# Four blocks of convolution and attention on one core: the order of the first transfers, |pos| and sign for the first pair on VectorE, the fourth block's norm and transpose ahead of the loop, the dense pair's late sums, and P7 before P3 in the projection

## The chip, the core and the metric

One core of a Trainium2 chip runs the whole program in one launch. The engines are TensorE (PE; its weight loads are listed as PEld), VectorE (DVE), ScalarE (ACT), GpSimd (POOL) and the queue engine SyncE (SP). The metric is the device time of one execution in microseconds; less is better. All arithmetic is in float32.

## What is computed

The input x is 2 x 512 x 32 x 32. Four layers follow one another, each adding to x.

Layer 0 is deformable attention with 8 heads and a dense pair. Per pair of heads (eight pairs: two images, four channel blocks of 128), cut to what matters here:

```python
q = gconv1x1(bn1(x))                              # per head 64 channels
off = tanh(gelu(depthwise_6x6_stride4(q)) @ pw) * 4
kv = grid_sample(bn1(x), key_grid + off)          # 64 keys; k, v = gconv1x1(kv)
pos = grid_q - grid_kv                            # 1024 queries x 64 keys x 2
bias = sign(pos) * log1p(abs(pos))
bias = relu(relu(bias @ w1 + b1) @ w2 + b2) @ w3 + b3
out = softmax(q @ k.T / 8 + bias) @ v
x = x + out_w @ out + out_b
x = x + mlp_w2 @ gelu(mlp_w1 @ bn2(x) + mlp_b1) + mlp_b2
```

Layer 1 is a linear attention. Layers 2 and 3 are group norm, attention with 8 heads over 1024 positions, and a projection that is added to x; layer 3's result is the output.

## The kernel before

x stays in on-chip memory as eight tiles of 128 x 1024 (`xs[b][t]`, image b, channel block t; called x00 to x13 below).

**Start (lines 72 to 177).** `prologue` issues the eight loads of x on SP's queue. `layer0` issues on ACT's queue, in this order: the first block of the q weights (`l0qkv`, L105), `cols` (all per-channel columns: norms, biases, the taps of the depthwise convolution, L106), `grid` (L107), `w2` (L109), the row of w3 (L254), the other k and v weights (L115), the other q weights (L116) and the output weights (L118). The program lets some of these issues wait for the landing of an earlier transfer (SP's third load of x waited 3.4 us for the first q weights), and what is queued behind such an issue on its engine waits as well.

The rest of the start is the first pair's chain (`offsets`, L317): its norm on VectorE (L450, wants x00 and `cols`), its q product (L469), copies of q into a padded tile (L478), the convolution by three engines at once (`first_conv`, L402: GpSimd makes 16 diagonal matrices, PE multiplies by them, ACT and VectorE take the other taps), gelu, tanh, and then `pos` (L367), ACT's Abs, Ln and Sign (L378 to L380) and the product `log` (L382). Into VectorE's queue between `pos` and `log` are placed the folding of |w3| into w2 (L276, L277) and the third part of the generator `last_weights`: `ends`, a matrix with the signs of w3 in four columns (L267, L270; the last product of the bias uses it), and the copy of the row numbers `ys` (L271; the first sampling uses it). Between the steps PE runs dummy products (`warm`, L147).

From `log` the first table is made (`table`, L553: two masked copies on VectorE, L579, spread over all partitions by PE, L586, then x by ACT, L595, and y by VectorE, L596), and from it the first hidden layer h (L618, VectorE). Before the loop, the transposes of the blocks 1 and 2 (normed ahead by GpSimd, L160) and the q of pair 1 are placed. ACT copies each transpose into an `att` tile; `sampled` (L483) takes it from there. For the other pairs `sampled` makes norm, transpose and copy itself, inside the loop (L493).

**Loop (L179 to L208).** 256 quads (16 heads x 8 groups of keys x 2). Each quad: PE multiplies h by w2 (L649, 64 passes), ACT applies Relu (L654), ACT, GpSimd and accumulating DMAs add signed parts, and the result goes into the last product (L681) two quads later. The next pair's steps and the softmax of finished heads are spread over the quads. PE, ACT, VectorE and GpSimd follow the order in which this code is written (`manual_schedule`).

**End of layer 0 and the dense pair.** The last head's softmax (`attend`, L689) alternates on PE with shares of the output projection (`share`, L227). `mlp0` (L824) begins with the norm of image 0 into seven blocks: `norm` makes four and `right_sums` (L803) forms four sums from them, two of which (L807, L808) feed only the products P7 and P4. This part stands outside a written-out order: a planner places its VectorE instructions into the queue by its own estimate of time. Then eight slabs follow in a written order, each with seven block products ("P1 P6 P2 P7 P5 P4 P3", then "P1 P3 P2 P6 P7 P5 P4") whose results VectorE adds up.

**Projection of layers 2 and 3 (`project`, L1572).** Seven products per image in the order P1 P2 P6 P5 P3 P7 P4, each in a place of two PSUM banks. After P6 GpSimd adds u to three blocks of x; P5 adds to two blocks, P3 to one, P7 to two, P4 to one, all on VectorE. In layer 3 each block is stored as soon as it is complete; for image 1, P4 is split into three pieces (L1596 to L1608).

Of the kernel before, what the change touches and what calls it, by code (L numbers as in the profile page):

```python
# [11 lines left out]
F32 = mybir.dt.float32  # L12
AF = mybir.ActivationFunctionType
# [5 lines left out]
P = 128  # L19
B, C, H, W = 2, 512, 32, 32  # L20
N = H * W
CT = C // P
# [32 lines left out]
class Net:  # L55
# [16 lines left out]
    def prologue(self, ctx: ExitStack):  # L72
        nc, io = self.nc, self.io
        const = self.const = self.pool(ctx, "const")
        xpool = self.pool(ctx, "x")
        self.cols = const.tile([P, NCOL], F32, tag="cols", name="cols")
        self.grid = const.tile([P, NGRID], F32, tag="grid", name="grid")
        x_in = io["x"].rearrange("b (t p) h w -> b t p (h w)", p=P)
        self.xs = []
        for b in range(B):  # L80
            self.xs.append([])
            for t in range(CT):
                xt = xpool.tile([P, N], F32, tag=f"x{b}{t}", name=f"x{b}{t}")
                nc.sync.dma_start(xt, x_in[b, t])
                self.xs[b].append(xt)
        self.ident = const.tile([P, P], F32, tag="ident", name="ident")
        make_identity(nc, self.ident)
# [10 lines left out]
    def layer0(self):  # L98
# [3 lines left out]
        with ExitStack() as ctx:  # L102
            keep = self.pool(ctx, "l0")
            self.l0qkv = keep.tile([P, 3, CT, P], F32, tag="qkv", name="qkv")
            nc.scalar.dma_start(self.l0qkv[:, 0, 0], io["l0_qkv"][:, 0, 0])  # L105
            nc.scalar.dma_start(self.cols, io["cols"])  # L106
            nc.scalar.dma_start(self.grid, io["grid"])  # L107
            self.l0w2 = keep.tile([P, P], F32, tag="w2", name="w2")
            nc.scalar.dma_start(self.l0w2, io["cpb_w2"])  # L109
# [31 lines left out]
            with self.tc.manual_schedule(engines=engines):  # L141
# [5 lines left out]
                def warm(n):  # L147
                    for _ in range(n):
                        nc.tensor.matmul(ones_ps[:, 0:P], lhsT=self.all, rhs=self.all, start=True, stop=True)

                warm(13)
                for n, _ in enumerate(self.offsets(pairs[0], 0, ps)):
                    if n == 1:
                        warm(5)
                    elif n == 2:
                        first_tr = self.turn(pairs[0], 0, ps)
                    elif n == 4:
                        warm(11)
                for t in (1, 2):
                    self.normed(pairs[t], t, True)  # L160
                pairs[0]["xT"] = self.fone.tile([P, NB, P], F32, tag="xnT", name="xnT00")
                nc.scalar.copy(pairs[0]["xT"], first_tr)
                front = [self.sampled(pairs[0], 0, ps)]
# [4 lines left out]


                att = [apool.tile([P, N], F32, tag=f"att{t}", name=f"att0_{t}") for t in range(CT)]  # L170
                for t in (1, 2):
                    tr = self.turn(pairs[t], t, ps)
                    pairs[t]["xT"] = att[t].rearrange("p (n c) -> p n c", c=P)
                    nc.scalar.copy(pairs[t]["xT"], tr)
                    if t == 1:
                        self.queries(pairs[1], 1, ps)
                del pairs[2]["xn"]
                held, self.join = [], None
                for i, (u, o, jj) in enumerate(quads):  # L179
                    self.jj = jj  # L180
# [66 lines left out]
    def last_weights(self, keep):  # L247

        nc = self.nc
        self.w3row = keep.tile([P, P], F32, tag="row", name="w3row")
        nc.scalar.dma_start(self.w3row, self.io["cpb_w3"].partition_broadcast(P))  # L254
        yield
        w3 = self.colr("w3r", 4)
        self.magb = keep.tile([P, 4], F32, tag="magb", name="magb")
        nc.vector.scalar_tensor_tensor(self.magb, w3, -1.0, w3, ALU.mult, ALU.max)
        nc.vector.tensor_tensor(self.magb, self.magb, self.colr("b2r", 4), ALU.mult)
        sign = keep.tile([P, 4], F32, tag="sign", name="sign")  # L260
        nc.vector.tensor_scalar(sign, w3, 0.0, 2.0, ALU.is_ge, ALU.mult)
        nc.vector.tensor_scalar(sign, sign, -1.0, None, ALU.add)
        self.flip = keep.tile([P, 3], F32, tag="flip", name="flip")
        nc.vector.tensor_tensor(self.flip, sign[:, 0:3], sign[:, 3:4].to_broadcast([P, 3]), ALU.mult)
        yield
        self.ends = keep.tile([P, 60], F32, tag="ends", name="ends")
        nc.vector.memset(self.ends, 0.0)  # L267
        for k in range(4):
            rows = slice(32 * k, 32 * k + 32)
            nc.vector.tensor_copy(self.ends[rows, 28 + k : 29 + k], sign[rows, 3:4])  # L270
        nc.vector.tensor_copy(self.ys, self.grid[:, G_Y : G_Y + NB])  # L271
        yield

# [43 lines left out]
    def offsets(self, m, bt, ps):  # L317
# [53 lines left out]
            ALU.subtract,  # L371
        )
        yield
        if bt == 0:
            self.fold_weights()
            next(self.weights)
        log = self.fpool.tile([P, 2, W], F32, tag="log", name=f"log{b}{t}")
        nc.scalar.activation(log, pos, AF.Abs)  # L378
        nc.scalar.activation(log, log, AF.Ln, bias=1.0)
        nc.scalar.activation(pos, pos, AF.Sign)  # L380
        yield
        nc.vector.tensor_tensor(log, log, pos, ALU.mult)  # L382
        logs = self.dram.tile([P, 2 * W], F32, tag="logs", name=f"logs{b}{t}")
        nc.sync.dma_start(logs, log.rearrange("p d x -> p (d x)"))
        spots = self.dram.tile([P, 2], F32, tag="spots", name=f"spots{b}{t}")
# [53 lines left out]
        nc.vector.tensor_tensor(conv, conv, acc, ALU.add)  # L439
        yield  # L440

    def normed(self, m, bt, ahead=False):
        nc = self.nc
        b, t = divmod(bt, CT)
        if ahead:
            xn = self.hid2.tile([P, N], F32, tag="h23", bufs=5, name=f"xn{b}{t}")
        else:
            xn = self.fone.tile([P, N], F32, tag="xn", name=f"xn{b}{t}")
        m["xn"] = xn
        (nc.gpsimd if ahead else nc.vector).tensor_scalar(  # L450
            xn, self.xs[b][t], self.s1[:, t : t + 1], self.col("bn1_b", t), ALU.mult, ALU.add
        )

# [99 lines left out]
    def table(self, u, o, pairs, tables):  # L553
# [14 lines left out]
        if u == 0 and o < 2:  # L568
# [8 lines left out]
            for d in range(2):  # L577
# [13 lines left out]
                    stop=True,  # L591
                )
                parts.append(got)
            x = tables["x"][:, :, i : i + 4, :]
            nc.scalar.activation(x, parts[0], AF.Identity, scale=self.col("cpb_w1", 0), bias=self.col("cpb_b1"))  # L595
            nc.vector.tensor_scalar(y, parts[1], self.col("cpb_w1", 1), None, ALU.mult)  # L596
# [205 lines left out]

    def right_sums(self, eng, r):  # L803

        eng.tensor_tensor(r[4], r[1], r[0], ALU.subtract)
        eng.tensor_tensor(r[5], r[3], r[4], ALU.subtract)
        eng.tensor_tensor(r[1], r[3], r[1], ALU.subtract)  # L807
        eng.tensor_tensor(r[6], r[2], r[5], ALU.subtract)  # L808

# [14 lines left out]
    def mlp0(self):  # L824
# [5 lines left out]
        with ExitStack() as ctx:  # L830
# [16 lines left out]
            def norm(b):  # L847

                r = [xpool.tile([P, 2, HF], F32, tag=f"r{i}", name=f"mx{b}{i}") for i in range(7)]
                for i in (0, 3, 2, 1):  # L850
                    for k in range(2):
# [7 lines left out]
                            ALU.add,  # L859
                        )  # L860
                        yield r
                self.right_sums(vec, r)
                yield r

            for xn in norm(0):
# [2 lines left out]
            with self.tc.manual_schedule(engines={getattr(mybir.EngineType, e) for e in ("PE", "Activation", "DVE")}):  # L868
                for n in range(B * CT):
# [11 lines left out]
                    for i, acc in self.seven("P1 P6 P2 P7 P5 P4 P3", ps, w1, lambda r, k: xn[r][:, k, :], f"m1_{n}"):  # L881
# [20 lines left out]
                                gelu(p, 1)  # L902
                        if i == "P5":
                            held = acc
                    for p in range(2):
                        self.right_sums(vec, h[p])
                    following = norm(1) if n == CT - 1 else iter(())
# [540 lines left out]
    def heads_bounded(self, k, ones, data, proj, out):  # L1448
# [7 lines left out]
        with ExitStack() as ctx:  # L1456
# [115 lines left out]
            def project(b):  # L1572
# [15 lines left out]

                us = ap2.tile([P, 2, HF], F32, tag="sum", name=f"pu{k}{b}")
                at = ("a", "b", "even", "a", "b", "even", "a") if b == 0 else ("odd", "even", "b", "odd", "even", "a", "b")  # L1590
                for which, spot in zip(("P1", "P2", "P6", "P5", "P3", "P7", "P4"), at):
                    a, ri = SEVEN[which]
                    acc = place(spot, f"pb{k}{b}{which}")
                    if out is not None and b == 1 and which == "P4":
# [307 lines left out]
```

## Time and profile before

| | us |
|---|---|
| three timed runs | 3351.06, 3352.95, 3353.19 |
| median | 3352.95 |
| the profiled execution's own time | 3351.15 |
| its span, first to last instruction | 3349.3 |
| PE busy | 3336.1 (100%) |
| VectorE busy | 2310.4 (69%) |
| GpSimd busy | 2176.0 (65%) |
| ACT busy | 2056.0 (61%) |
| granted TensorE clock, mean | 1.000 |

The span and all times in the profile come from one profiled execution; what lies outside the span makes 1.85 us of that execution. Times of instructions are counted from the start of the span. Lines of a timeline have start, duration, engine and line of code, operation, output <- input, shape and count, and in brackets how long the engine was idle before and what ended that. A list of waits has total, number and longest wait. An engine named with a q (ACTq, SPq) is its queue of issues. The PE's busy time includes overlapping of successive matmuls. The idle time of PE in the span is 3349.3 - 3336.1 = 13.2 us.

By stage: the start with the first pair's chain takes the first 23 us; the loop runs to about 2005; layer 0's last softmax and projection end at 2033; the dense pair ends at 2417; layer 1 at 2481; layer 2 at 2914; layer 3 takes the rest.

### The profile page before, as it was taken

What the parts mean: (1) busy time and instruction counts of PE and PEld (TensorE: products, weight loads), DVE (VectorE), ACT (ScalarE), POOL (GpSimd) and SP (SyncE); (2) the same over time, 40 slices, a digit from 0 to 9 for tenths busy, and PEclk for the clock granted to TensorE, in tenths of its full rate; (3) what the DMA queues carried; (4) which work ended last, traced back from release to release, by engine and by line L of the source; (5) the groups of instructions that cost most, each with busy time, mean ns of one, the idle gap of its engine ahead of it and who ended that gap; (6) DMA issues with size and microseconds to landing.
All of it is one profiled execution on the core that took longest, in us unless ns stands there. A gap on an engine that the chain in (4) does not pass through costs nothing.

```text
span 3349.3 us, 60380 instructions
## 1 busy us (share of the span) xinstructions
PE 3336.1 (100%) x25318; PEld 1242.6 (37%) x25318; DVE 2310.4 (69%) x2521; ACT 2056.0 (61%) x2173; POOL 2176.0 (65%) x1665
## 2 busy tenths in 40 slices
PE   9999999999999999999999999999999999999999
PEld 4333333333333333333333334444565533455333
DVE  6777777767766677777766665564565578755787
ACT  7887887887886688887888771111121466213662
POOL 6887878877877677878878874333323447634475
PEclk9999999999999999999999999999999999999999
DMA  7777877877777577777888762111000100000001
GB/s 178 158 160 152 160 158 154 160 156 158 160 154 143 119 157 150 161 157 152 160 172 162 159 136 104 38 51 38 1 1 0 38 2 1 14 0 14 1 1 52
DMA packets 102674, 342.67 MB, mean 102 GB/s; under 512 B 12657, under 2 KB 14833, under 8 KB 99313
## 3 DMA queue, kind: packets, MB, share of 16 engines
q0 software_dynamic: 73296, 266.90, 40.8%
q1 hardware_dynamic: 27936, 69.68, 7.2%
q8 instruction: 203, 3.33, 0.4%
q10 hardware_dynamic: 1152, 2.06, 0.2%
q14 instruction: 87, 0.70, 0.1%
HBM read 67.27 MB, written 4.46 MB: 21 GB/s over the span
## 4 chain that ended last, share of the span: by engine, by line
PE 96%; DVE 1%; POOL 1%; issue 1%; DMA 0%; ACT 0%; ACTq 0%; POOLq 0%; DVEq 0%
PE hp L649 51%; PE s L1482 7%; PE o L1511 7%; PE sim L681 3%; PE qk30P L1260 1%; PE qk20P L1260 1%; PE qk31P L1260 1%; PE m_6P L819 1%; PE m_5P L819 1%; PE m_3P L819 1%; PE m_1P L819 1%; PE m_0P L819 1%; PE qk21P L1260 1%; PE m_7P L819 1%; PE m_4P L819 1%; PE m_2P L819 1%
## 5 line engine op out<-in xcount | busy, mean ns | idle before, releaser
L649 PE MATMUL hp<-h,w 128*32 128x512 f32 x16384 | 1794.9, 593 | 0.3 <-ACT h L654 0.3
L618 DVE CUSTOM_DVE_ANT_1 h<-tx,bank 128x1024 f32<-128x1024 f32 (+1 forms) x1028 | 1181.0, 1212 | 310.2 <-PE hp L649 239.1
L654 ACT ACTIVATE h<-hp,magb 128x1024 f32<-128x1024 f32 x1024 | 1120.9, 1111 | 371.3 <-PE hp L649 365.1
L649 PEld LDWEIGHTS hp<-h,w 128*32 128x32 f32 x16384 | 526.9, 110 | 1199.0 <-issue 1148.0
L641 POOL DMA_DIRECT2D h<-h x509 | 451.4, 1024 | 365.6 <-ACT h L660 308.8
L667 POOL TENSOR_TENSOR h<-h,h 128x1024 f32<-128x1024 f32 x255 | 610.3, 2393 | 21.3
L665 POOL TENSOR_SCALAR h<-h,flip 128x1024 f32<-128x1024 f32 x256 | 448.4, 1751 | 0.9 <-ACT h L654 0.9
L1486 ACT ACTIVATE e<-s 128x1024 f32<-128x1024 f32 x256 | 261.8, 1024 | 155.5 <-PE s L1482 151.7
L656 ACT ACTIVATE h<-h,flip 128x1024 f32<-128x1024 f32 x256 | 291.4, 1138 | 0.0
L1482 PE MATMUL s<-q,k 64*64 64x512 f32 x2048 | 265.2, 589 | 0.0
L1511 PE MATMUL o<-e,v 64*64 64x512 f32 x2048 | 265.1, 589 | 0.0
L1493 POOL TENSOR_TENSOR some<-some,e 128x1024 f32<-128x1024 f32 x64 | 160.8, 2513 | 42.5 <-ACT e L1486 38.7
L1491 POOL TENSOR_TENSOR some<-e,e 128x1024 f32<-128x1024 f32 x32 | 75.8, 2367 | 157.8 <-DVE sum L1500 125.6
L658 POOL TENSOR_SCALAR h<-h,flip 128x1024 f32<-128x1024 f32 x128 | 142.9, 1116 | 45.4 <-ACT h L654 44.7
L660 ACT ACTIVATE h<-h,flip 128x1024 f32<-128x1024 f32 x128 | 145.7, 1138 | 0.0
L681 PE MATMUL sim<-h,ends 128*32 128x512 f32 x1024 | 133.3, 592 | 0.0
L1511 PEld LDWEIGHTS o<-e,v 64*64 64x64 f32 x2048 | 78.3, 133 | 141.4 <-issue 135.1
L1482 PEld LDWEIGHTS s<-q,k 64*64 64x64 f32 x2048 | 78.1, 133 | 141.0 <-issue 115.5
L797 POOL TENSOR_TENSOR mlp_w<-mlp_w 128x512 f32<-128x512 f32 x16 | 22.3, 1393 | 161.6 <-DMA mlp_w<-in_mlp_w 161.5
L1496 DVE TENSOR_TENSOR sum<-e,e 128x1024 f32<-128x1024 f32 x32 | 57.4, 1792 | 99.8 <-ACT e L1486 99.8
L878 ACT ACTIVATE mh<-mh,cols 128x512 f32<-128x512 f32 x64 | 46.2, 722 | 124.2 <-DVE mh L896 65.5
L1534 DVE RECIPROCAL r<-r 128x512 f32<-128x512 f32 x32 | 107.3, 3353 | 1.1
(545 smaller groups left out, 3313.6 us busy)
## 6 DMA issues: line engine op xcount, KB each, us to landing
h<-h POOLq DMA_DIRECT2D x509, 512.0 KB, 6.4
lb<-logs SPq DMA_DIRECT2D x63, 512.0 KB, 5.2
mlp_w<-in_mlp_w SPq DMA_DIRECT2D x16, 1024.0 KB, 4.9
x<-in_x SPq DMA_DIRECT2D x8, 512.0 KB, 9.8
qkw<-in_l_qk SPq DMA_DIRECT2D x2, 2048.0 KB, 8.3
out<-x SPq DMA_DIRECT2D x15, 256.0 KB, 2.1
vw<-in_l_v SPq DMA_DIRECT2D x2, 1024.0 KB, 8.0
projw<-in_l_proj SPq DMA_DIRECT2D x2, 1024.0 KB, 4.6
```

Source lines behind the costliest of these rows:

```text
L618: self.nc.vector._custom_dve(TENSOR_ADD_SAT, out=h1[r][:, k, cut, :], in0=x[:, jj, 2 * r + k, :].unsqueeze(1).to_broadcast([P, H // parts, ...
L641: nc.gpsimd.dma_start(to, what, accum_op=ALU.add)
L649: nc.tensor.matmul(hp[rows, cut], lhsT=self.l0w2[:, 32 * q : 32 * q + 32], rhs=h1[k][:, cut], start=True, stop=True)
L654: nc.scalar.activation(y, hp, AF.Relu, bias=self.magb[:, q : q + 1])
L656: nc.scalar.activation(ys[0], ys[0], AF.Copy, scale=self.flip[:, 0:1])
L665: nc.gpsimd.tensor_scalar(y, y, self.flip[:, 2:3], 1.0, ALU.mult, ALU.mult)
L667: (nc.vector if final else nc.gpsimd).tensor_tensor(y, y, ys[2], ALU.add)
L681: nc.tensor.matmul(sims[u][at : at + 32, :], lhsT=self.ends[:, 28 - 4 * o : 60 - 4 * o], rhs=z[jj][:, h * HF : (h + 1) * HF], start=(o == ...
L819: self.nc.tensor.matmul(acc[p], lhsT=w[:, a, k, p * P : (p + 1) * P], rhs=right(r, k), start=k == 0, stop=k == 1)
L1482: nc.tensor.matmul(s[halves[c], par, :], lhsT=ks[p][rows, at : at + DH], rhs=qs[p][rows, cut], start=True, stop=True)
L1486: nc.scalar.activation(e, s, AF.Exp, scale=DH**-0.5)
L1511: nc.tensor.matmul(o[halves[par], r, :], lhsT=v[n // 2][rows, n % 2, at : at + DH], rhs=e[rows, par, :], start=(n == 0), stop=(n == NB - 1),)
```

## The change

- `cols` becomes the first transfer on ACT's queue. The loads of x move from `prologue` into `layer0`, still on SP's queue, and the first block of the q weights goes to SP, between the loads of x00 and x01.
- For the first pair, |pos| is max(-pos, pos) on VectorE, and the sign is made there as 2 (pos >= 0), used as (that - 1) times the logarithm; ACT keeps Ln alone. `ends` (a memset and four copies) goes to GpSimd, and the `ys` copy becomes a step of its own, taken when the second table is made.
- The first run of dummy products has 11 instead of 13. The norms of the blocks 1 and 2 stand earlier in the program on GpSimd.
- Block 3 is normed ahead as well, on VectorE, inside the first table; its transpose and copy go before the loop with those of 1 and 2, and pair 1's q products come after the three transposes.
- The last two sums of the dense pair's first image move from the norm to behind P6 of the first slab.
- In `project`, P7 comes before P3; the places keep their order.

```diff
--- before.py
+++ after.py
@@ -75,13 +75,11 @@
         xpool = self.pool(ctx, "x")
         self.cols = const.tile([P, NCOL], F32, tag="cols", name="cols")
         self.grid = const.tile([P, NGRID], F32, tag="grid", name="grid")
-        x_in = io["x"].rearrange("b (t p) h w -> b t p (h w)", p=P)
         self.xs = []
         for b in range(B):
             self.xs.append([])
             for t in range(CT):
                 xt = xpool.tile([P, N], F32, tag=f"x{b}{t}", name=f"x{b}{t}")
-                nc.sync.dma_start(xt, x_in[b, t])
                 self.xs[b].append(xt)
         self.ident = const.tile([P, P], F32, tag="ident", name="ident")
         make_identity(nc, self.ident)
@@ -102,8 +100,13 @@
         with ExitStack() as ctx:
             keep = self.pool(ctx, "l0")
             self.l0qkv = keep.tile([P, 3, CT, P], F32, tag="qkv", name="qkv")
-            nc.scalar.dma_start(self.l0qkv[:, 0, 0], io["l0_qkv"][:, 0, 0])
+            x_in = io["x"].rearrange("b (t p) h w -> b t p (h w)", p=P)
             nc.scalar.dma_start(self.cols, io["cols"])
+            for bt in range(BP):
+                b, t = divmod(bt, CT)
+                nc.sync.dma_start(self.xs[b][t], x_in[b, t])
+                if bt == 0:
+                    nc.sync.dma_start(self.l0qkv[:, 0, 0], io["l0_qkv"][:, 0, 0])
             nc.scalar.dma_start(self.grid, io["grid"])
             self.l0w2 = keep.tile([P, P], F32, tag="w2", name="w2")
             nc.scalar.dma_start(self.l0w2, io["cpb_w2"])
@@ -148,16 +151,16 @@
                     for _ in range(n):
                         nc.tensor.matmul(ones_ps[:, 0:P], lhsT=self.all, rhs=self.all, start=True, stop=True)
 
-                warm(13)
+                warm(11)
                 for n, _ in enumerate(self.offsets(pairs[0], 0, ps)):
                     if n == 1:
                         warm(5)
                     elif n == 2:
                         first_tr = self.turn(pairs[0], 0, ps)
+                        for t in (1, 2):
+                            self.normed(pairs[t], t, nc.gpsimd)
                     elif n == 4:
                         warm(11)
-                for t in (1, 2):
-                    self.normed(pairs[t], t, True)
                 pairs[0]["xT"] = self.fone.tile([P, NB, P], F32, tag="xnT", name="xnT00")
                 nc.scalar.copy(pairs[0]["xT"], first_tr)
                 front = [self.sampled(pairs[0], 0, ps)]
@@ -168,13 +171,12 @@
 
 
                 att = [apool.tile([P, N], F32, tag=f"att{t}", name=f"att0_{t}") for t in range(CT)]
-                for t in (1, 2):
+                for t in range(1, CT):
                     tr = self.turn(pairs[t], t, ps)
                     pairs[t]["xT"] = att[t].rearrange("p (n c) -> p n c", c=P)
                     nc.scalar.copy(pairs[t]["xT"], tr)
-                    if t == 1:
-                        self.queries(pairs[1], 1, ps)
-                del pairs[2]["xn"]
+                self.queries(pairs[1], 1, ps)
+                del pairs[2]["xn"], pairs[3]["xn"]
                 held, self.join = [], None
                 for i, (u, o, jj) in enumerate(quads):
                     self.jj = jj
@@ -264,10 +266,11 @@
         nc.vector.tensor_tensor(self.flip, sign[:, 0:3], sign[:, 3:4].to_broadcast([P, 3]), ALU.mult)
         yield
         self.ends = keep.tile([P, 60], F32, tag="ends", name="ends")
-        nc.vector.memset(self.ends, 0.0)
+        nc.gpsimd.memset(self.ends, 0.0)
         for k in range(4):
             rows = slice(32 * k, 32 * k + 32)
-            nc.vector.tensor_copy(self.ends[rows, 28 + k : 29 + k], sign[rows, 3:4])
+            nc.gpsimd.tensor_copy(self.ends[rows, 28 + k : 29 + k], sign[rows, 3:4])
+        yield
         nc.vector.tensor_copy(self.ys, self.grid[:, G_Y : G_Y + NB])
         yield
 
@@ -371,15 +374,23 @@
             ALU.subtract,
         )
         yield
+        log = self.fpool.tile([P, 2, W], F32, tag="log", name=f"log{b}{t}")
         if bt == 0:
+
+            nc.vector.scalar_tensor_tensor(log, pos, -1.0, pos, ALU.mult, ALU.max)
+            nc.vector.tensor_scalar(pos, pos, 0.0, 2.0, ALU.is_ge, ALU.mult)
             self.fold_weights()
             next(self.weights)
-        log = self.fpool.tile([P, 2, W], F32, tag="log", name=f"log{b}{t}")
-        nc.scalar.activation(log, pos, AF.Abs)
-        nc.scalar.activation(log, log, AF.Ln, bias=1.0)
-        nc.scalar.activation(pos, pos, AF.Sign)
-        yield
-        nc.vector.tensor_tensor(log, log, pos, ALU.mult)
+            nc.scalar.activation(log, log, AF.Ln, bias=1.0)
+        else:
+            nc.scalar.activation(log, pos, AF.Abs)
+            nc.scalar.activation(log, log, AF.Ln, bias=1.0)
+            nc.scalar.activation(pos, pos, AF.Sign)
+        yield
+        if bt == 0:
+            nc.vector.scalar_tensor_tensor(log, pos, -1.0, log, ALU.add, ALU.mult)
+        else:
+            nc.vector.tensor_tensor(log, log, pos, ALU.mult)
         logs = self.dram.tile([P, 2 * W], F32, tag="logs", name=f"logs{b}{t}")
         nc.sync.dma_start(logs, log.rearrange("p d x -> p (d x)"))
         spots = self.dram.tile([P, 2], F32, tag="spots", name=f"spots{b}{t}")
@@ -439,7 +450,7 @@
         nc.vector.tensor_tensor(conv, conv, acc, ALU.add)
         yield
 
-    def normed(self, m, bt, ahead=False):
+    def normed(self, m, bt, ahead=None):
         nc = self.nc
         b, t = divmod(bt, CT)
         if ahead:
@@ -447,7 +458,7 @@
         else:
             xn = self.fone.tile([P, N], F32, tag="xn", name=f"xn{b}{t}")
         m["xn"] = xn
-        (nc.gpsimd if ahead else nc.vector).tensor_scalar(
+        (ahead or nc.vector).tensor_scalar(
             xn, self.xs[b][t], self.s1[:, t : t + 1], self.col("bn1_b", t), ALU.mult, ALU.add
         )
 
@@ -591,6 +602,10 @@
                     stop=True,
                 )
                 parts.append(got)
+            if o == 0:
+                self.normed(pairs[3], 3, nc.vector)
+            else:
+                next(self.weights)
             x = tables["x"][:, :, i : i + 4, :]
             nc.scalar.activation(x, parts[0], AF.Identity, scale=self.col("cpb_w1", 0), bias=self.col("cpb_b1"))
             nc.vector.tensor_scalar(y, parts[1], self.col("cpb_w1", 1), None, ALU.mult)
@@ -802,8 +817,16 @@
 
     def right_sums(self, eng, r):
 
+        self.first_sums(eng, r)
+        self.second_sums(eng, r)
+
+    @staticmethod
+    def first_sums(eng, r):
         eng.tensor_tensor(r[4], r[1], r[0], ALU.subtract)
         eng.tensor_tensor(r[5], r[3], r[4], ALU.subtract)
+
+    @staticmethod
+    def second_sums(eng, r):
         eng.tensor_tensor(r[1], r[3], r[1], ALU.subtract)
         eng.tensor_tensor(r[6], r[2], r[5], ALU.subtract)
 
@@ -859,7 +882,9 @@
                             ALU.add,
                         )
                         yield r
-                self.right_sums(vec, r)
+                self.first_sums(vec, r)
+                if b > 0:
+                    self.second_sums(vec, r)
                 yield r
 
             for xn in norm(0):
@@ -902,6 +927,8 @@
                                 gelu(p, 1)
                         if i == "P5":
                             held = acc
+                        if i == "P6" and n == 0:
+                            self.second_sums(vec, xn)
                     for p in range(2):
                         self.right_sums(vec, h[p])
                     following = norm(1) if n == CT - 1 else iter(())
@@ -1588,7 +1615,7 @@
 
                 us = ap2.tile([P, 2, HF], F32, tag="sum", name=f"pu{k}{b}")
                 at = ("a", "b", "even", "a", "b", "even", "a") if b == 0 else ("odd", "even", "b", "odd", "even", "a", "b")
-                for which, spot in zip(("P1", "P2", "P6", "P5", "P3", "P7", "P4"), at):
+                for which, spot in zip(("P1", "P2", "P6", "P5", "P7", "P3", "P4"), at):
                     a, ri = SEVEN[which]
                     acc = place(spot, f"pb{k}{b}{which}")
                     if out is not None and b == 1 and which == "P4":
```

## The prediction

> **What bounds the kernel now.** I read the page's busy times and chain first, then the list of waits of the matmul engine, then timelines of the places which those waits name: the first 35 us, a stretch inside the long loop, the end of layer 0, and the last 10 us.
>
> ```profile
> PE 3336.1 (100%) x25318; PEld 1242.6 (37%) x25318; DVE 2310.4 (69%) x2521; ACT 2056.0 (61%) x2173; POOL 2176.0 (65%) x1665
> ...
> PE 96%; DVE 1%; POOL 1%; issue 1%; DMA 0%; ACT 0%; ACTq 0%; POOLq 0%; DVEq 0%
> ```
> PE is without matmuls for only 3349.3 - 3336.1 = 13.2 us. A change gains only where it shortens those 13 us, moves PE work into a stretch where PE waits anyway, or shortens the head and the foot of the span. The list of waits of PE names the stretches:
>
> ```profile
> PE bank L725 <- DVE e L721: 1.8, 1, 1.8
> PE qk30P L1260 <- ACT xn L1435: 1.6, 1, 1.6
> PE ones_ps L149 <- POOL all L112: 1.1, 1, 1.1
> PE q L469 <- DVE xn L450: 1.1, 1, 1.1
> PE pb21P L1613 <- DVE xn L1443: 0.6, 1, 0.6
> ```
> The start hides more than this list: 26 of its passes are dummies (L149), and the first real product waits for VectorE piece by piece. Timeline of the start (start, duration):
>
> ```profile
> 1.18 0.45 ACTq L106 DMA_DIRECT2D cols<-in_cols  x1
> ...
> 6.50 0.17 DVE L95 TENSOR_SCALAR bn1s<-cols 128x4 f32<-128x4 f32 x1 [6.50 <-DMA cols<-in_cols]
> 6.71 0.81 DVE L450 TENSOR_SCALAR xn<-x,bn1s,cols 128x1024 f32<-128x1024 f32 x1
> ...
> 17.77 0.24 ACT L380 ACTIVATE pos<-pos 128x64 f32<-128x64 f32 x1
> ...
> 18.07 0.23 DVE L382 TENSOR_TENSOR log<-log,pos 128x64 f32<-128x64 f32 x1
> ...
> 20.67 9.40 DVE L618 CUSTOM_DVE_ANT_1 h<-tx,bank 128x512 f32<-128x512 f32 x12
> ...
> 22.85 8.95 PE L649 MATMUL hp<-h,w 128*32 128x512 f32 x64
> ```
> Read: cols, not x, lets the first norm go. The log follows 0.06 us after ACT's Sign and 0.04 us after VectorE's own queue, so both hold it. The 64 passes take 8.95 us where the loop gives 64 of them 7.07 us (the row that begins at 660.99): PE waits there for h.
>
> **The change, part by part.**
>
> *cols first (start).* cols is issued at 0.74 and not at 1.18. Its issue alone is worth 0.44. The nearest row for its new place is the transfer that had this place before: qkv, 64 KB, first on ACT's queue, landed 4.2 us after its issue, at 4.94, as x00 (4.0 us, at 4.74). cols is 70 KB. A rule speaks against counting more than 0.44: the Trainium skill, "DMA: Bandwidth & Descriptors", section "Issuing engines are not separate DMA queues", says that transfers of several engines interleave on the same 16 engines and that another issuer saves only issue time. By the rule the sum has 0.4 here, by the row 6.48 - 4.94 = 1.54. I take the row: cols lost its time behind qkv and among x01's packets (1.18 to 6.28), not in bandwidth. Upper end 1.74 (landing with x00). qkv now follows x00 on SP, where x01 landed at 6.28; it is an eighth of x01, so between 4.8 and 6.28, and is needed when xn ends (5.17 + 0.81 = 5.98). ACT's table load (6.87, 1.28) stands behind ACT's DMA issues, of which the last (ow, issued 6.50) waited for an earlier landing; if it comes to wait for one near 6.7 again, ACT's half of the q copies starts a us late. Dummies: 13 cost 5.38; with 11 they end by 5.9, before q. Starts lie 0.21 apart until about 5.8 and then 0.11, although the granted clock reads 1.00 throughout. The skill, "TensorE: Matmul & The Clock Gate", section "What's actually happening", asks about 3.4 us of activity in a free-running window; the trace shows 4.7. By the rule 11 dummies (22 passes x 0.21 = 4.7) suffice amply; by the row they just do, and a later window would run the q products (1.09 us) at half rate, +0.8 on the path at most. So 1.5, ends 0.4 and 1.74.
>
> *|pos| and sign on VectorE.* Before: pos ends 16.58, fold 0.6, memset and four copies 17.07 to 17.83, ys to 18.03, log 18.07. After: two more 128x64 operations (about 0.2 apiece net, like L382 and L365), fold 0.6, then log; memset and copies go to Pool, ys to the next table. ACT has Ln alone after its table load: 17.34 + 0.26, log at about 17.65. Gain 0.4 (0.3 to 0.5). Pool is idle 16.54 us up to 31.91, so its five operations and its wait for sign (15.60) cost nothing; only the edge memsets of the second qpad queue behind them, wanted at 21.96. The two norms on Pool keep their place behind the 16 diagonals. The ys copy falls in VectorE's 2.65 us wait before L596 of the second table (33.39).
>
> *Fourth block ahead.* Added at the start: one 0.81 us norm on VectorE, eight transposes, one 1.01 us ACT copy. The norm goes between L579 and L596, where VectorE was idle 0.95; it needs x03, landed 15.94, at about 17.2 of the new time. If x03 were later, y, h and all behind wait one for one. The transposes (0.87 to 1.02 for eight) put the first hp pass at 22.0 where it would be 21.0, but its last h piece comes from VectorE at 25.5 less the shift, so the product ends the same. The copy goes ahead of the q copies (as the order of the transposes now does); ACT was idle 1.32 before its first Relu (26.69), 0.3 is left. Removed: the same transposes in the loop, where PE never waits:
>
> ```profile
> 668.85 1.09 PE L550 MATMUL tr<-ident,xn 128*128 128x128 f32 x8
> 669.88 2.35 PE L649 MATMUL hp<-h,w 128*32 128x512 f32 x20
> ```
> 669.88 - 668.85 = 1.03. Gain 1.0; ends 0 (all of it comes back as a stall at the start) and 1.0. The norm for the fourth q stays in the loop.
>
> *The dense pair's late sums.* They now stand inside the last softmax of layer 0 on VectorE's queue:
>
> ```profile
> 2008.58 1.22 DVE L806 TENSOR_TENSOR mx<-mx,mx 128x1024 f32<-128x1024 f32 x1
> 2009.71 1.22 DVE L807 TENSOR_TENSOR mx<-mx,mx 128x1024 f32<-128x1024 f32 x1
> 2010.85 0.69 DVE L713 TENSOR_REDUCE st<-bank 128x8 f32<-128x512 f32 x1
> 2011.45 1.79 DVE L808 TENSOR_TENSOR mx<-mx,mx 128x1024 f32<-128x1024 f32 x1
> 2013.16 0.68 DVE L714 TENSOR_TENSOR e<-bank,st 128x512 f32<-128x512 f32 x1
> ...
> 2015.50 0.76 DVE L721 TENSOR_TENSOR e<-e,st 128x512 f32<-128x512 f32 x1
> ```
> The transposes that L713 reads end at 2009.38; without L807 it starts at 2009.75 (-1.1), and without L808 L714 follows at once (-1.6). e is ready 2.7 earlier, at 2013.6. PE has its shares of the projection until 2014.53, so only its whole wait of 1.79 goes; what is late next is PE itself. Moved to: behind P6's two additions, 2040.9. P7's matmuls, after three products of 3.46 us from 2033.05, want the third sum at 2043.4; it ends at 2042.1, at its slowest (2.29) at 2043.2. Queued behind: P2's additions, up to 1.8 late, with eight PSUM banks and gaps of 1.0 between additions to catch up. Cost nothing; 0.5 if both are slow. Gain 1.8 (1.2 to 2.1: the program's order on VectorE is not written by hand here, and the filler may stand otherwise).
>
> *P7 before P3.* PE's order of work and its places stay as full. At the end of layer 2 PE waits for P4's additions (to 2914.46) whatever precedes them, so nothing there. At the very end VectorE reaches P4's first piece a us late:
>
> ```profile
> 3342.54 1.89 PE L1599 MATMUL pb<-v,projw 128*128 128x256 f32 x8
> ...
> 3343.54 0.74 DVE L1607 SCALAR_TENSOR_TENSOR x<-pb31P,cols,x 128x512 f32<-128x512 f32 x1
> 3344.20 0.87 DVE L1607 SCALAR_TENSOR_TENSOR x<-pb,cols,x 128x256 f32<-128x256 f32 x2
> ```
> PE ends at 3344.43; the last addition started at 3344.59 and could start at 3344.46: 0.1 (0 to 0.3). P7's additions wait for Pool's last, 3338.9, and start 3337.6: covered by the next product.
>
> **Sum.** 1.5 + 0.4 + 1.0 + 1.8 + 0.1 = 4.8 us. The profiled execution took 3351.15 (span 3349.3 and 1.85 around it): 3346.3. The three timed runs have a median of 3352.95, so 3348.1 there: 0.14% less, inside the 0.2% which is about what a measurement of this kernel can tell from no change.
>
> **Rivals.**
> - *The start keeps its time* (0.25): cols gains its issue time only, ACT's table load is held by a DMA issue, or q runs before the clock is released. 0.4 + 0.4 + 1.0 + 1.8 + 0.1 = 3.7: 3349.2. For it: ACT's queue did wait so before (ow). Against: the qkv row.
> - *A wait in place of one removed* (0.12): the fourth copy or norm holds the first Relu or h (0.3 of slack, x03's landing), or filler takes the freed place in the softmax. Some 2 us less: 3350.
> - *More than counted* (0.15): VectorE's fewer fillers also free L704, and PE's small waits around it (0.34, 0.38) and part of the start's second stall (31.7 to 33.7) go: 2 us more, 3346.
> - *Slower* (0.03): two dummies too few. From the point where passes still run at half rate past 18 us (5.8 now), q (+0.8), the convolution's products (3.97, +2.4 less 0.4 slack) and 4 us of transposes and q double on the path: +7 against 4.8, 3355. Against it: 11 dummies last as long as the slow phase does.
>
> My forecast has 0.45. Faster by over 0.2% means below 3346.2: the upper half of the third rival and scatter (the runs spread over 2.1), 0.15. The range 3345.3 to 3351.0 takes in the rivals but the last.
>
> **What would show it.** Right: cols landing near 5.0, q near 6.1, log near 15.8 to 16.2, L618 first at 18.7 to 19; no transposes at the fourth pair's place in the loop; no wait at L725; L807 and L808 behind L887. Wrong: q after 7, ACT's table load after 6.5, a VectorE wait for x03, a first Relu that follows ACT's copies directly, a PE wait at P7 in the first dense slab, or PE's waits adding to over 9 us.

## The result and the profile after

The kernel after takes 3346.16 us (median of 20 runs, 3345.68 to 3348.48), the kernel before, timed beside it, 3351.36 (20 runs, 3350.71 to 3353.24). The ratio is 0.9984 with an interval of 0.9978 to 0.9990: 5.2 us less, 0.16%: a small gain, but one that the interval sets apart from none. The sum made against the profiled execution (3346.3) is almost this time. The forecast of 3348.1 stood higher because it started from the median of three runs, 3352.95, and 20 runs of the same kernel have a median 1.6 us lower.

In both kernels some executions take about 2 us longer than the rest (6 of 20 before, 3 of 20 after), and the profiled execution of the kernel after is one of them: it took 3348.48, its mean granted clock is 0.999, and 1.7 us of it are lost in layer 1, as shown at the end. Stages are therefore compared one by one.

The page's busy times and chain, after:

```profile
PE 3336.4 (100%) x25314; PEld 1242.0 (37%) x25314; DVE 2313.9 (69%) x2519; ACT 2056.6 (61%) x2171; POOL 2178.0 (65%) x1670
...
PE 97%; DVE 1%; POOL 1%; issue 1%; ACT 0%; DMA 0%; POOLq 0%; DVEq 0%; ACTq 0%
```

PE is without matmuls for 3346.7 - 3336.4 = 10.3 us, where it was 13.2. Its busy time would have fallen too, but holds the 1.7 us lost in layer 1. PE's list of waits, after:

```profile
PE qk30P L1287 <- issue: 1.5, 1, 1.5
PE ones_ps L152 <- POOL all L115: 1.1, 1, 1.1
PE pb21P L1640 <- DVE xn L1470: 0.6, 1, 0.6
PE bank L723 <- DVE ss L719: 0.3, 1, 0.3
```

The wait for e (1.8), the wait of q (1.1) and the first wait of lb_ps, the table's spread, (0.5) are gone; the others stand within 0.1 of what they were, and none took a place that was freed. The q product before:

```profile
7.58 1.09 PE L469 MATMUL q<-xn,qkv 64*64 64x512 f32 x8 [1.06 <-DVE xn L450]
```

The start, from timelines of the kernel after:

```profile
0.74 0.41 ACTq L104 DMA_DIRECT2D cols<-in_cols  x1
4.80 0.17 DVE L93 TENSOR_SCALAR bn1s<-cols 128x4 f32<-128x4 f32 x1 [4.80 <-DMA cols<-in_cols]
5.01 0.81 DVE L461 TENSOR_SCALAR xn<-x,bn1s,cols 128x1024 f32<-128x1024 f32 x1
...
6.13 1.51 PE L480 MATMUL q<-xn,qkv 64*64 64x512 f32 x8
...
16.58 0.23 DVE L391 SCALAR_TENSOR_TENSOR log<-pos,log 128x64 f32<-128x64 f32 x1
...
17.52 0.81 DVE L461 TENSOR_SCALAR xn<-x,bn1s,cols 128x1024 f32<-128x1024 f32 x1
```

The norm starts 1.70 us earlier (6.71 to 5.01), but q only 1.45 (7.58 to 6.13), because the dummies ahead of it last beyond the norm's end at 5.82. And it takes 1.51 where it took 1.09. The logarithm's product comes at 16.58 where it came at 18.07, and h starts at 19.19 where it started at 20.67. Both come later than the prediction's signs (15.8 to 16.2, and 18.7 to 19), because the first transfers brought the convolution forward by 1.0 and not by 1.5. The fourth block's norm (17.52) stands in a gap of VectorE and waits for nothing. The softmax before the dense pair: PE's line before, which still has the wait, then VectorE and PE after.

```profile
2016.32 0.66 PE L725 MATMUL bank<-ident,e 128*128 128x128 f32 x4 [1.79 <-DVE e L721]
```

```profile
2007.13 0.68 DVE L728 TENSOR_REDUCE st<-bank 128x8 f32<-128x512 f32 x1
2007.85 0.69 DVE L729 TENSOR_TENSOR e<-bank,st 128x512 f32<-128x512 f32 x1
...
2010.20 1.06 DVE L736 TENSOR_TENSOR e<-e,st 128x512 f32<-128x512 f32 x1
...
2006.63 5.32 PE L236 MATMUL ob<-att,ow 128*128 128x512 f32 x12
2011.79 0.60 PE L740 MATMUL bank<-ident,e 128*128 128x128 f32 x4
```

No sum stands between the reduction and the subtraction. e ends at 2011.26 and PE comes to it at 2011.79 from its own work, with no wait in brackets: PE is late next, as forecast. The sums run at 2036.21 and 2037.34, and no matmul of the dense pair waits for them.

### The profile page after: what moved, and what is told of

The parts are those of the page before. It is cut to its first block, busy times and chain, and to the rows that moved or that the text cites. A ratio compares the mean times of both kernels' runs of the same rounds, so it can differ in the third digit from the quotient of the medians.

```text
span 3346.7 us, 60378 instructions
## 1 busy us (share of the span) xinstructions
PE 3336.4 (100%) x25314; PEld 1242.0 (37%) x25314; DVE 2313.9 (69%) x2519; ACT 2056.6 (61%) x2171; POOL 2178.0 (65%) x1670
## 4 chain that ended last, share of the span: by engine, by line
PE 97%; DVE 1%; POOL 1%; issue 1%; ACT 0%; DMA 0%; POOLq 0%; DVEq 0%; ACTq 0%
PE hp L664 52%; PE s L1509 7%; PE o L1538 7%; PE sim L696 3%; PE qk30P L1287 1%; PE qk20P L1287 1%; PE m_3P L842 1%; PE qk31P L1287 1%; PE m_7P L842 1%; PE m_5P L842 1%; PE m_2P L842 1%; PE m_0P L842 1%; PE qk21P L1287 1%; PE m_6P L842 1%; PE m_1P L842 1%; PE m_4P L842 1%
```

## The experiments

All times are medians; "after" is 3346.16. The kernel before took 3351.26, 3351.07 and 3351.20 beside the three groups of runs. To compare single stages in the traces, four distances are used: the convolution's first product (10.24 before, 9.22 after); from there to the first product of the first table, lb_ps (8.66, 8.20); from that to the first transposes of the last softmax, L708 before and L723 after (1989.82, 1988.72); and from those to the first product of the dense pair (24.33, 22.32). Each kernel has one profile, so a distance is that of one execution. The diffs are cut to the lines that matter.

**The transfers alone.** The kernel before, with the new order of the first transfers and 11 dummies, and nothing else of the change:

```diff
-            nc.scalar.dma_start(self.l0qkv[:, 0, 0], io["l0_qkv"][:, 0, 0])
             nc.scalar.dma_start(self.cols, io["cols"])
+            for bt in range(BP):
+                b, t = divmod(bt, CT)
+                nc.sync.dma_start(self.xs[b][t], x_in[b, t])
+                if bt == 0:
+                    nc.sync.dma_start(self.l0qkv[:, 0, 0], io["l0_qkv"][:, 0, 0])
-                warm(13)
+                warm(11)
```

> The kernel before with one step alone: cols first on ACT, the first q weights on SP between x00 and x01, 11 dummies. Theory (packet order, not issue time, held cols): cols lands near 4.8, the first norm starts near 5.0 (6.71 before), the log near 17.0 to 17.1 (18.07 before), the second quad's first pass 1.0 to 1.1 us before 33.66; time 1.0 us under the kernel before. Rival (only the issue time counts): cols near 6.0, the norm near 6.3, 0.4 us. Second rival (the q products always run at half rate when they start near 6.1): gain 1.0 although the norm is 1.7 earlier; if they run at full rate, 1.5.

3350.05, ratio 0.9995 (0.9986 to 1.0003): 1.2 us less, with an interval that includes no change. In its trace the norm starts at 4.91, 1.80 earlier than before, the convolution's first product comes at 9.32, 0.92 earlier, and the second distance is 8.65, unchanged. The rule's 0.44 is too little, the full 1.5 is not reached: in this execution q took 1.61 us, which is what the second rival has.

**The fourth block back in the loop.** The kernel after, without its norm in the first table and its transpose ahead:

```diff
-                for t in range(1, CT):
+                for t in (1, 2):
-            if o == 0:
-                self.normed(pairs[3], 3, nc.vector)
-            else:
+            if o == 1:
                 next(self.weights)
```

> The changed kernel with the fourth block's norm, transpose and copy in the loop again. Theory: the start keeps its times (second quad's first pass at 32.2, within 0.1), eight transposes stand in the loop near 670, and everything behind them is 1.03 us later than in the changed kernel. Rival (the transposes at the start cost something there): the second quad's first pass comes earlier than 32.1 by what they cost, and the net is under 1.0. Second rival (the loop hides them): nothing lost, 0.

3347.74, 1.6 more than after. A timeline of its loop has the eight transposes again:

```profile
667.15 1.09 PE L561 MATMUL tr<-ident,xn 128*128 128x128 f32 x8
668.17 13.94 PE L662 MATMUL hp<-h,w 128*32 128x512 f32 x128
```

668.17 - 667.15 = 1.02 is their price, and the third distance is 1989.89, 1.17 more than after. In its profile another 0.4 is in layer 2, which the edit doesn't touch: from the first product of layer 2 to that of layer 3 it takes 433.35 us, the kernel after 432.96 and all other profiles up to 433.00, and a wait of PE for VectorE's xn is 1.0 where it is 0.6 after. Why is open. So the step itself is worth 1.0 to 1.2, and it costs nothing at the start: the second quad's first product comes 14.75 us behind lb_ps in both kernels.

**The late sums back.** The kernel after, with all four sums in the norm:

```diff
-                if b > 0:
-                    self.second_sums(vec, r)
+                self.second_sums(vec, r)
-                        if i == "P6" and n == 0:
-                            self.second_sums(vec, xn)
```

> The changed kernel with all four sums of the dense pair's first image in the norm again. Theory: the two late sums stand inside the softmax again, the wait of PE at the last transposes returns with 1.8, the dense pair's first pass is 1.8 to 2.0 us later than in the changed kernel and so is the end. Rival (the time comes from another order of the fillers, or is given back in the dense pair): under 1.0.

3348.28, 2.1 more than after. PE's list of waits has the removed line again:

```profile
PE bank L740 <- DVE e L736: 2.0, 1, 2.0
```

Its fourth distance is 24.52, 2.20 more than after. The profile gives the wait and the medians give the same 2 us.

**P3 before P7 again.** The kernel after, with

```diff
-("P1", "P2", "P6", "P5", "P7", "P3", "P4")
+("P1", "P2", "P6", "P5", "P3", "P7", "P4")
```

> The changed kernel with P3 before P7 again in the projection. Theory: the last addition starts 0.16 after the last pass in place of 0.03, time 0.1 us more, which timing can hardly tell; nothing moves between layers 2 and 3. Rival (the order also frees a place for layer 3): layer 3's first pass moves by 0.5 or more.

3346.24: 0.1 more, which these runs can't tell from nothing. The trace shows more. The last lines of VectorE, in the kernel after:

```profile
3339.80 0.75 DVE L1634 SCALAR_TENSOR_TENSOR x<-pb31P,cols,x 128x512 f32<-128x512 f32 x1 [0.31 <-PE pb31P L1626]
...
3341.53 0.48 DVE L1634 SCALAR_TENSOR_TENSOR x<-pb,cols,x 128x256 f32<-128x256 f32 x1 [0.38 <-PE pb L1626]
```

VectorE now waits for PE before the first and the last piece, where before it ran late without a gap. The last addition comes 3.06 us earlier than before and PE's last pieces 2.94: 0.12 gained there, and this run's trace gives it back. But it is not seen at the end of the span. From layer 3's first product to that end the ten profiles with P7 first take 434.48 to 435.09 us, 434.76 on average, and the three with P3 first 434.67 to 434.95, 434.77 on average. The last store took 2.8 to 3.4 us from its issue to its landing in the ten, and 2.3 to 2.5 in the three; why is not known.

**|pos| and sign on ACT again**, and **ends on VectorE again**, each from the kernel after:

```diff
-            nc.vector.scalar_tensor_tensor(log, pos, -1.0, pos, ALU.mult, ALU.max)
-            nc.vector.tensor_scalar(pos, pos, 0.0, 2.0, ALU.is_ge, ALU.mult)
+        nc.scalar.activation(log, pos, AF.Abs)
+        nc.scalar.activation(log, log, AF.Ln, bias=1.0)
+        nc.scalar.activation(pos, pos, AF.Sign)
```

```diff
-        nc.gpsimd.memset(self.ends, 0.0)
+        nc.vector.memset(self.ends, 0.0)
-            nc.gpsimd.tensor_copy(self.ends[rows, 28 + k : 29 + k], sign[rows, 3:4])
+            nc.vector.tensor_copy(self.ends[rows, 28 + k : 29 + k], sign[rows, 3:4])
```

> The changed kernel with |pos| and sign on ACT again for the first pair; the ends matrix stays on GpSimd. Theory (both queues held the log): ACT's Sign ends 0.45 us later than the Ln does in the changed kernel, the log follows it, and the first h starts near 19.6 in place of 19.19; time 0.4 more. Rival (VectorE's copies alone held it): h at 19.2, nothing lost.

> The changed kernel with the memset and the four copies of the ends matrix on VectorE again, ahead of the log; |pos| and sign stay on VectorE. Theory: VectorE's queue now holds the log by about 0.7 to 0.8 us (the memset and copies took 0.76): log near 17.3, h near 19.9, time 0.7 more, longer than with all of it undone (0.47). Rival (ACT alone held it): h at 19.2.

3346.62 and 3347.01, 0.5 and 0.85 more than after. The second distance tells it without the scatter of the rest: 8.64 and 8.93, against 8.20 after and 8.66 before. Either half undone takes back nearly all of the 0.46 or more: ACT and VectorE both held the logarithm, and both have to be relieved. With only ends back, VectorE's queue carries more than before the change. (Its logarithm's product comes at 16.76, earlier than expected, because the convolution of this execution starts at 8.66; the loss is in the distance.)

**Thirteen dummies, and four.** The kernel after, with `warm(13)` and with `warm(4)` in place of `warm(11)`.

> The changed kernel with 13 first dummies. Theory (the clock, not the count, matters): the dummies end near 6.5, q starts 0.4 later but at full rate (1.09 in place of 1.51), so the copies of q start within 0.1 of 7.7 and the time is the same. Rival (the removed dummies gain by themselves): 0.4 more.

> The changed kernel with 4 first dummies. Theory (activity releases the clock): the passes stay at half rate through q and into the convolution; q takes 1.5 or more, the convolution's passes up to 6.4 in place of 3.97, the second quad's first pass 0.5 to 3 us after 32.17, time 0.5 to 3 more. Rival (release comes at a fixed time after the start): nothing lost. The slower rival of the prediction wants 7 lost here.

3346.24 and 3347.35: two more change nothing that these runs can tell, seven fewer cost 1.2. Here is the start with four, from PE's timeline:

```profile
5.87 1.98 PE L480 MATMUL q<-xn,qkv 64*64 64x512 f32 x8 [2.66 <-DVE xn L461]
7.79 2.50 PE L152 MATMUL ones_ps<-all 128*128 128x128 f32 x10
10.08 4.35 PE L425 MATMUL conv_ps<-qpad,diag 128*128 128x64 f32 x32
```

All of q, the next dummies and the convolution's first products run at half rate, until about 11, some 5 us from q's start. The rival's 7 us needed half rate past 18; here it ends long before, though only 8 dummy passes went ahead of q. One of the 20 executions took 3352.55, 5.2 more than their median, at a mean granted clock of 1.000. It was not profiled, so with four dummies a single execution near the rival's price is not excluded; with eleven none of the 20 lies more than 2.4 above the median.

**The first flip on GpSimd.** The kernel after; in the first quad, where ACT's two flips and Relus hold the second quad back and GpSimd is idle, GpSimd takes the second flip:

```diff
-                if jj == 1:
+                if jj == 1 or (u, o) == (0, 0):
```

> The changed kernel, and in the first quad GpSimd in place of ACT applies the sign to the second part. Theory (from 26.9 to 32.1 the chain is ACT's: Relu, two sign copies, two Relus, and PE waits for the last): ACT is free 1.04 earlier, the last Relu then waits for PE's product (30.2), and the second quad's first pass comes 0.7 us earlier than 32.17; time 0.7 less. Rival (the product's own passes or the tables hold it): 0.

3345.37, ratio to before 0.9983 (0.9976 to 0.9991). The second quad's first product comes 14.16 us behind lb_ps, not 14.75: 0.6 of the 0.8 is seen there. It is the lowest time of the study.

**All four sums late.** The last kernel, with the first two sums written behind P1:

```diff
-                self.first_sums(vec, r)
+                        if i == "P1" and n == 0:
+                            self.first_sums(vec, xn)
```

> As the run before, and the first two sums of the dense pair's first image also leave the norm, for behind P1 of the first slab. Theory: the softmax's first step no longer waits for a sum, PE's wait of 0.34 before its transposes goes, another 0.3 us; P6 wants the second sum 3.46 us after P1 starts, and it is ready just then. Rival: P6 waits for it, up to 1 us lost, and the run is slower than the one before.

3345.87. It doesn't test what it was meant to: in the built program the instructions of PE, VectorE, ACT and GpSimd stand in the same order as in the kernel with the flip, and the trace has the two sums at 2003.57 and 2005.37, before the slab as ever. So it is a repeat, and shows how far two medians of one program lie apart: 0.5 us. The gain of the flip is then 0.3 to 0.8 by medians and 0.6 by the trace, and differences under 0.5 above are read from the traces.

**More narrow products in layer 1.** To try a cause for the 1.7 us lost in layer 1 (last section), the 64 products of 65 columns of the first image were made twice; no value changes:

```diff
-                    for n in range(NB):
+                    for n in [*range(NB)] * (2 if b == 0 else 1):
```

> The changed kernel with the 64 narrow passes (65 columns) of layer 1's product of keys and x for the first image done twice, so 7.3 us more of them. They change no value. Theory (a window of the clock gate in which few columns flow lowers the clock, and some executions meet it in layer 1: 3 of 20 of the changed kernel are 2 us longer, with granted clock 0.77 at 2442 to 2446): [...]nearly every execution has it: granted clock under 0.9 there, time 7.3 + 1.7 to 3.4 more, without two groups of times. Rival (the two groups come from elsewhere or from chance): 7.3 more and about one execution in six 2 us longer.

3353.26 (3352.65 to 3353.89, 13 runs), 7.1 more than after: what the added products cost (in the trace the doubled products take 14.46 where they took 7.31). No execution shows a lower mean clock, and in the trace it reads 1.00 throughout layer 1. The theory that a longer stretch of such products brings the clock down has fallen. The rival's one execution in six did not come either, but 0 of 13 can be chance.

## Why the prediction was right, step by step

| step | predicted | in the traces | by an experiment's median |
|---|---|---|---|
| cols first | 1.5 | 1.02 (0.9 to 1.8) | 1.2 |
| abs, sign, ends | 0.4 | 0.46 | 0.5 and 0.85 |
| fourth block | 1.0 | 1.0 to 1.2 | 1.6, of it 0.4 in layer 2 |
| late sums | 1.8 | 2.0 | 2.1 |
| P7 before P3 | 0.1 | 0.12 at the last addition, nothing at the end | 0.1, not told from nothing |
| sum | 4.8 | 4.6 without the last | (whole) 5.2 |

With 1.25 for cols, the average over the profiles given below, the traces' sum is 4.8; the remaining 0.4 is not placed, and is less than two medians of one program lay apart.

**cols first: the mechanism was right, the term too large.** The transfer did what the qkv row said and not what the rule said: cols landed 4.0 us after its issue instead of 5.3, and the norm started 1.70 earlier, against 0.44 by the rule on issuing engines. Where cols stood in the queues was worth more than when it was issued; whether it was freed from qkv ahead of it or from x01's packets was not separated. The lost part is the next link. I took from one profile that the dummies' half rate ends at 5.8, let 11 of them end by 5.9, and set the risk for q aside. But the instant differs from one execution to the next, and the free-running window of the rule cited there promises no fixed one, so "amply" claimed too much. The kernel with the flip on GpSimd and that with more products in layer 1 have the same start and the same 11 dummies as the kernel after; the PE timeline of the first, then the dummies of the second:

```profile
1.14 4.53 PE L152 MATMUL ones_ps<-all 128*128 128x128 f32 x22 [1.14 <-POOL all L115]
5.87 1.09 PE L480 MATMUL q<-xn,qkv 64*64 64x512 f32 x8 [0.21 <-DVE xn L461]
```

```profile
1.14 4.16 PE L152 MATMUL ones_ps<-all 128*128 128x128 f32 x22 [1.14 <-POOL all L115]
```

Here the 22 passes take 4.53 and 4.16: the rate rose while they ran, q waits for xn (0.21 in the first) and runs in 1.09. In the profile of the kernel after they take 5.06, to 6.20, so q starts about 0.25 later, and it begins at half rate: 1.51, another 0.42. Over the eleven profiles with the new transfers and at least 11 dummies, the convolution starts between 8.47 and 9.32, at 8.99 on average: the step gives 1.25 on average, in single executions from 0.92 to 1.77. That thirteen dummies make no difference may come from this: where the rate rises late, q would stand behind them about as long as it now runs slow. The one profile with thirteen can't show it, since there the rate rose early, at about 5.2.

**|pos| and sign.** 0.46 for 0.4. In the kernel after VectorE's folding ends at 16.58 and ACT's Ln at 16.55, and log follows at once: both hold it still.

**Fourth block.** Right, with no price at the start: the first Relu had 0.60 us of ACT's idle time before it, more than the 0.3 worked out.

**Late sums.** Under-sized by 0.2: the wait removed was 1.79 in the list, and the distance between the two groups of transposes around it shrank from 7.60 to 5.65, by 1.95. The row counts the wait from the end of the share ahead of it. Without the wait PE does not stand until that end: the transposes start at 2011.79, 0.16 before the share ends (2006.63 + 5.32 = 2011.95). The sums' new place cost nothing: P2's additions came behind them, and no PE wait is listed in the dense pair.

**The end.** The addition moved as forecast, but the end of the span did not follow, so the term of 0.1 is not shown. The wait between layers 2 and 3 stayed (1.6 before, 1.5 after).

**The rivals.** A wait in place of one removed did not come. Of more than counted nothing came: the wait of 0.3 before L723 stood. Slower did not come in any of the 20 executions, and with four dummies its price was 1.2 in the median and not 7. The first rival happened in part and in some executions, by its third cause (q before the full rate): in the profile of the kernel after, 1.02 was left of the step's 1.5, where the rival left 0.4.

**The number.** What failed is the base: I set the sum against a median of three runs, two of which were among the longer executions. Against the 20 runs' median of 3351.36 the same sum gives 3346.6. That this comes so near to 3346.16 is in part luck: the terms for cols and for the late sums were off by 0.2 to 0.5 in opposite directions.

## What to carry to other kernels

When PE is at 100%, sum the waits of its list stage by stage and look for each at what VectorE's or ACT's queue holds right in front of the awaited instruction; moving it behind a point of slack gave the wait in full here. A small chain held by two engines gained only when both were relieved. And a step that meets a clock limit should be sized over several profiles: one profile shows one draw.

## What was not expected of the hardware

**The instant of full rate.** From PE's first pass (1.14) it took about 3 to 6 us until passes followed at 0.11 instead of 0.21, in kernels with the same start: at about 4.2 in the earliest profile and 7.0 in the latest, by the counts of passes in each half microsecond. The granted clock reads 1.00 all that time. The Trainium skill ("TensorE: Matmul & The Clock Gate", "What's actually happening") has a free-running window of about 3.4 us, so that the instant depends on its phase, but gives the variation as half a microsecond to either side, though it also tells there of a kernel with 6, 11 or 14 slow matmuls by that phase; here it spans 2.8 us from end to end. What sets the instant in an execution is not shown.

**A low clock inside layer 1.** Windows of the kernel after; the columns are PE, PEld, DVE, ACT and POOL busy with their instructions, then the granted clock:

```profile
2435.00:2440.00 5.00, 5.00 (x47) 5.00 (x47) 4.54 (x10) 0.22 (x1) 0.00 (x0) 1.00 0.00 0
2440.00:2445.00 5.00, 5.00 (x51) 5.00 (x51) 1.27 (x4) 0.38 (x1) 0.00 (x0) 0.91 0.01 3
2445.00:2450.00 5.00, 5.00 (x13) 1.68 (x12) 0.13 (x1) 0.58 (x1) 0.00 (x0) 0.75 0.00 0
2450.00:2455.00 5.00, 5.00 (x36) 4.04 (x35) 2.85 (x6) 0.68 (x2) 0.00 (x0) 1.00 0.00 0
```

PE is busy throughout, with many short products and then eight long ones, and still the clock falls to 0.75. Eight products of 512 columns take 4.91 us where they take 3.60 before. From the dense pair's first product to that of layer 2 this execution needs 450.21 us and the kernel before 448.52: 1.69 lost. The kernel with the transfers alone lost the same 1.69 in its profile, and in the profile of the kernel with the sums back the clock read 0.50 from about 11.4 to 18.3, which made the second distance 10.60 where it is 8.20. These are the three profiles with a mean clock of 0.999. In the runs of the kernel after and of the experiments, 22 of 215 executions have a mean clock under 1.000, and all 22 are 1.0 to 2.5 us above their kernel's median; of the others only the 3352.55 with four dummies is more than 0.9 above. So the longer executions are those with a lowered clock, but where it fell in those without a profile is not known. What sets off the drop stays open; more of the short products (the last experiment) didn't.
